# Attention over four images on one core: loads and issues of the start, of each image's first units and of the last group rearranged

## The chip, the cores and the metric

The kernel runs on one core of a Trainium2 chip. The core has five engines with a queue each: PE (TensorE, the matrix engine), ACT (ScalarE), DVE (VectorE), POOL (GpSimd) and SP (SyncE, which here only starts transfers). Transfers (DMAs) started from ACT, SP and POOL share 16 DMA engines. The metric is the device time of one execution in microseconds (us); the median of ten runs is taken.

## The reference

Four images of 64 x 64 points with 256 channels go through one attention layer. `x`, the weights and the result are float32.

```python
B, W, H, C = x.shape            # 4, 64, 64, 256
N = W * H                       # 4096
q = einsum('bwhc,cd->bwhd', x, Wq) + bq      # 128 wide
k = einsum('bwhc,cd->bwhd', x, Wk) + bk      # 128 wide
v = einsum('bwhc,cd->bwhd', x, Wv) + bv      # 256 wide
pq, pk, pv = (t.reshape(B, -1, N) for t in (q, k, v))
energy = einsum('bcn,bcm->bnm', pq, pk)
out = einsum('bcm,bnm->bcn', pv, softmax(energy, axis=-1))
return gamma * out.reshape(B, W, H, C) + x
```

The reshapes make the 4096 columns n and m out of a part of the points and the channels together, which is why q and k pass through DRAM once: they are written in one order and read in another.

## The kernel before

**Exactness.** The large products are made of fp32r matmuls[...]. So each operand is cut into parts: `h` (upper), `l` (rest) and `d` (a scaled combination of both), likewise `vh`, `vl`, `vd` for v and three parts in one tile for q and for k. `halved` (line 245 and on) cuts q or k: one ACT instruction (line 247) and two DVE instructions (line 249). Column 256 of `vh` and `vl` holds ones, so that the accumulators `a0` and `a1`, 258 wide, also collect the softmax's denominator.

**Setting up (lines 84 to 101, 189, 208).** POOL makes `ident`, DVE makes `ones`; ACT's queue starts all weight loads: `wqk_sb` twice, `wv_sb`, `bqk_sb` twice, `bv_sb` twice, `gam`. ACT then scales the bias of v (line 189). DVE puts the ones into `vh` and `vl` (line 208).

**Projection, steps i = 0 to 15 of an image.** A step takes 256 columns: `transposed` (four PE transposes of the x tile, copied from PSUM by ACT, line 129), `project_qk` (eight matmuls, line 136; bias added by DVE, line 145; q parts `qd` and the cut k `kf` stored to DRAM by POOL) and `project_v` of the step before (eight matmuls, line 157; two biased copies by ACT, line 166; `vh` by ACT, line 267; `vl` and `vd` by DVE, line 270). x tiles are loaded by SP, two steps ahead, into three buffers. From step 8 on `begin` brings in the attention's first work: at step 8 `load_q` (SP), at step 9 `halve_q`, at steps 8, 9 and 10 the first three `load_k` (POOL, 768 KB each), from step 10 on half a unit of `energy` per step, at steps 12 to 15 `join` and `upper` of units 0 and 1.

**Attention, units u = 0 to 127 of an image.** A group g has 256 columns n; a unit t, one of eight of a group, takes 512 columns m. For a unit, `energy` makes scores in two halves into the banks `sa` and `sb` (two of each; twelve matmuls, line 303), and ACT takes exponentials of both (line 307, tiles `x` and `y`). `join` multiplies them on DVE (line 317), `upper` makes `h` on ACT (line 322), `halves` makes `l` (line 328) and `d` (line 331) on DVE. `attend` (line 351) multiplies `h`, `l`, `d` with `vh`, `vl`, `vd` into `a0`, `a1` and `bb`: 24 matmuls. Unit t uses the v blocks that steps t and t + 8 made.

The program is written out in the order in which each engine runs it; the framework adds the waits but does not reorder inside the main part. In the loop over units, energies run three units ahead (`LOOK = 3`), `join` and `upper` two units and `halves` one unit ahead:

```python
for k in range(2):
    if ahead < STEPS:
        energy(b, ahead, k)
    if k == 0 and u + 2 < STEPS:
        join(b, u + 2)
        upper(b, u + 2)
load_k(b, ahead + 2)
proceed()
if u + 1 < STEPS:
    halves(b, u + 1)
```

Ahead of the loop stand `halves(b, 0)` and then `project_v(b, NI - 1)`, after the whole of step 15.

**End of a group.** `whole` takes the denominators (line 368) and joins `o` (copied from `bb` by ACT, line 361) with the accumulators (line 371). `finish` is cut into pieces by `yield`; each `proceed()` runs one piece: factors (lines 378, 379) and scaling by ACT (line 381), later four transposes (line 389), later the addition to the x tile (line 393) and the store by POOL (line 394). At the end of an image `while active: proceed()` runs all that is left, ahead of the next image's third transpose.

**End of the program.** All denominators are checked (lines 474 to 481): if one is out of range, a flag sends the program into a general version behind `tc.If`, which does not run with these inputs. All engines read the flag and jump over it.

Of the kernel before, what the change touches and what calls it, by code (L numbers as in the profile page):

```python
# [9 lines left out]
F32 = mybir.dt.float32  # L10
F32R = mybir.dt.float32r
I32 = mybir.dt.int32
AF = mybir.ActivationFunctionType
# [7 lines left out]
def kernel(  # L21
# [67 lines left out]
    wqk_sb = const.tile([P, KC, 2 * C2], F32, name="wqk_sb")  # L89
    nc.scalar.dma_start(wqk_sb[:, :, :C2], wq.rearrange("(k p) d -> p k d", p=P))  # L90
    nc.scalar.dma_start(wqk_sb[:, :, C2:], wk.rearrange("(k p) d -> p k d", p=P))
    wv_sb = const.tile([P, KC, C], F32, name="wv_sb")
    nc.scalar.dma_start(wv_sb, wv.rearrange("(k p) e -> p k e", p=P))
    bqk_sb = const.tile([P, 2 * C2], F32, name="bqk_sb")
    nc.scalar.dma_start(bqk_sb[:, :C2], bq.partition_broadcast(P))
    nc.scalar.dma_start(bqk_sb[:, C2:], bk.partition_broadcast(P))
    bv_sb = const.tile([P, KC], F32, name="bv_sb")
    for eh in range(KC):
        nc.scalar.dma_start(bv_sb[:, eh : eh + 1], bv[eh * P : (eh + 1) * P].unsqueeze(1))
    gam = const.tile([P, 1], F32, name="gam")  # L100
    nc.scalar.dma_start(gam, gamma.partition_broadcast(P))

    class Projection:

# [72 lines left out]
    NU = NM // 4  # L177
    STEPS = NG * NU
    LOOK = 3
    E = 2.0**-12  # L180


    UPPER = 1.0 - 2.0**-13

    again = const.tile([P, 1], I32, name="again")

    zall = const.tile([P, B * NG, NJ], F32, name="zall")
    bv4_sb = const.tile([P, KC], F32, name="bv4_sb")
    nc.scalar.mul(bv4_sb, bv_sb, 1.0 / E)

    with ExitStack() as fast:
        fast.enter_context(tc.manual_schedule())
# [8 lines left out]
        ps_t = pool("ps_t", 1, space=PSUM)  # L201


        vh = qkv.tile([P, NM, C + 2], F32R, tag="vh", name="vh")
        vl = qkv.tile([P, NM, C + 2], F32R, tag="vl", name="vl")
        vd = qkv.tile([P, NM, C], F32R, tag="vd", name="vd")
        for t in (vh, vl):
            nc.vector.tensor_copy(t[:, :, C:], ones[:, : 2 * NM].rearrange("p (m t) -> p m t", t=2))

        images, qd, kf, units, loads, now = [], {}, {}, {}, {}, {}  # L210

# [41 lines left out]
        def project_qk(b, i):  # L253
            images[b].qk(i)
            x = now["qk"]
            for s in range(2):
                nc.gpsimd.dma_start(qd[b, i // 2 + NG // 2 * s][:, i % 2, :], x[:, s, :C2])
            f = kpool.tile([P, 2, 3, P], F32R, tag="f", name=f"f_{b}_{i}", bufs=2)
            halved(f, x[:, :, C2:])
            nc.gpsimd.dma_start(kf[b, i // 2][:, i % 2], f.rearrange("p s j d -> p s (j d)"))  # L260

        def project_v(b, i):
            images[b].v(i)
            v4 = now["v4"]
            m = slice(2 * i, 2 * i + 2)
            h = vh[:, m, :C]
            nc.scalar.activation(h, v4, AF.Identity, scale=UPPER * E)  # L267

            for t, f in ((vl, 1.0 / E), (vd, 1.0 / E + 1.0)):
                nc.vector.scalar_tensor_tensor(  # L270
                    t[:, m, :C], h.bitcast(F32), -f, v4, ALU.mult, ALU.add
                )
# [6 lines left out]
        def halve_q(b, g):  # L279
            t = work.tile([P, NJ, 3, P], F32R, tag="q", name=f"q_{b}_{g}")  # L280
            halved(t, loads.pop((b, "qr", g)))
            loads[b, "q", g] = t

        def load_k(b, u):
            if u < STEPS:
                t = kpool.tile([P, 4, 3, P], F32R, tag="k", name=f"k_{b}_{u}")
                nc.gpsimd.dma_start(t.rearrange("p (i s) f d -> p i s (f d)", s=2), kf[b, u % NU])  # L287
                loads[b, "k", u] = t
# [47 lines left out]
        def attend(b, u, j):  # L336
            g, t = divmod(u, NU)
            if t == j == 0:
                now["acc"] = [
                    ps_o.tile([P, C + 2], F32, tag=f"a{j}", name=f"a{j}_{b}_{g}")  # L340
                    for j in range(NJ)
                ]
                now["bb"] = ps_o.tile([P, NJ, C], F32, tag="bb", name=f"bb_{b}_{g}")
            h, l, d = units[b, u]
            a, bb = now["acc"][j], now["bb"]
            n = slice(j * P, (j + 1) * P)
            for out_, left, right in ((a, h, vh), (a, l, vl), (bb[:, j, :], d, vd)):
                for i in range(4):
                    m = 2 * t + i // 2 + NI * (i % 2)

                    nc.tensor.matmul(  # L351
                        out_,
                        left[:, i, n],
                        right[:, m, :],
                        start=(t == i == 0 and (left is h or left is d and j == 0)),
                        stop=(t == NU - 1 and i == 3 and left is not h),
                        skip_group_check=True,
                    )
            if t == NU - 1 and j == NJ - 1:
                now["o"] = work.tile([P, NJ, C], F32, tag="o", name=f"o_{b}_{g}")  # L360
                nc.scalar.copy(now["o"], bb)

        def whole(b, g):

            o = now["o"]
            for j in range(NJ):
                a = now["acc"][j]
                nc.vector.tensor_copy(zall[:, b * NG + g, j : j + 1], a[:, C : C + 1])
            for j in range(NJ):
                a = now["acc"][j]  # L370
                nc.vector.scalar_tensor_tensor(
                    o[:, j, :], a[:, :C], 1.0 + E, o[:, j, :], ALU.mult, ALU.add
                )

        def finish(b, g, o, xr):
            yield
            r = work.tile([P, NJ], F32, tag="r", name=f"r_{b}_{g}")
            nc.vector.reciprocal(r, zall[:, b * NG + g, :])
            nc.vector.tensor_tensor(r, r, gam.to_broadcast([P, NJ]), ALU.mult)  # L379
            for j in range(NJ):  # L380
                nc.scalar.activation(  # L381
                    o[:, j, :], o[:, j, :], AF.Identity, scale=r[:, j : j + 1]
                )
            yield
            yield
            tp = ps_t.tile([P, 2, NB], F32, tag="t", name=f"ot_{b}_{g}")
            for s in range(2):
                for j in range(NJ):
                    nc.tensor.transpose(  # L389
                        tp[:, s, j * P : (j + 1) * P], o[:, j, s * P : (s + 1) * P], ident  # L390
                    )
            yield
            nc.vector.tensor_tensor(xr, xr, tp, ALU.add)
            nc.gpsimd.dma_start(ov[b, g], xr)

        def begin(b, i):

            if i == 8:
                load_q(b, 0)
            if i == 9:  # L400
                halve_q(b, 0)
            if 8 <= i <= 10:
                load_k(b, i - 8)
            if i >= 10:
                energy(b, (i - 10) // 2, i % 2)
            if i in (12, 14):
                join(b, i // 2 - 6)
            if i in (13, 15):
                upper(b, i // 2 - 6)
                load_k(b, i // 2 - 3)  # L410

        image(0)
        for b in range(B):
# [6 lines left out]
            for i in range(1, NI):  # L420
                if i == 3:
                    now["banks"] = outputs
                if i + 1 < NI:
                    pr.transposed(i + 1)
                begin(b, i)
                project_qk(b, i)
                project_v(b, i - 1)
                proceed()
            halves(b, 0)
            project_v(b, NI - 1)  # L430
            for u in range(STEPS):
                g, t = divmod(u, NU)
# [22 lines left out]
                    halves(b, u + 1)  # L455
                if ahead // NU + 1 < NG and ahead % NU == 5:
                    halve_q(b, ahead // NU + 1)
                for j in range(NJ):
                    attend(b, u, j)
                if t == NU - 1:  # L460
                    whole(b, g)
                    start(finish(b, g, now["o"], loads.pop((b, "x", g))))
                proceed()
            if b + 1 < B:
                images[b + 1].transposed(1)
                project_qk(b + 1, 0)
            while active:
                proceed()


    zs = const.tile([P, 1], F32, name="zs")
    zf = zall.rearrange("p n j -> p (n j)")
    ok = const.tile([P, B * NG * NJ], F32, name="ok")
    nc.vector.tensor_scalar(ok, zf, Z_LOW, None, ALU.is_ge)
    nc.vector.scalar_tensor_tensor(ok, zf, Z_HIGH, ok, ALU.is_le, ALU.mult)
    nc.vector.tensor_reduce(zs, ok, AX.X, ALU.min)
    nc.vector.tensor_scalar(zs, zs, 0.5, None, ALU.is_lt)
    with tc.tile_pool(name="ps_z", bufs=1, space=PSUM) as ps_z:
        zp = ps_z.tile([P, 1], F32, name="zp")
        nc.tensor.matmul(zp, ones, zs, start=True, stop=True)  # L480
        nc.vector.tensor_copy(again, zp)

    NB = 512
    NG = N // NB
# [132 lines left out]
```

## Time and profile before

| what | value |
|---|---|
| median of 10 runs | 2520.88 us (2518.69 to 2523.57) |
| the profiled execution's own time | 2521.07 us |
| its span, first to last instruction | 2518.9 us |
| PE busy | 2486.1 us, 99% |
| DVE busy | 2103.6 us, 84% |
| ACT busy | 1806.4 us, 72% |
| POOL busy | 425.1 us, 17% |
| mean granted PE clock | 0.998 |
| DMA moved | 498.92 MB, 198 GB/s |

The profile shows one execution. A row of the timeline gives the start in us from the span's start, the duration, the engine, the line in the kernel, the instruction, result and operands, the number of instructions put together in the row, and in brackets the idle time before it with what ended that. `PEld` is PE's loading of weights, which runs beside its matmuls. A row of the waits gives the engine and line that waited, what it waited for, and the sum, the number and the longest of these waits. The engine's busy rows divide the span into 40 equal slices and give the busy share in tenths. The time of the run is a little longer than the span, by what lies around the first and the last instruction.

### The profile page before, as it was taken

The page shows a single profiled execution, that of the slowest core. Times are in us where ns is not written, and L with a number is a line of the kernel's source. Part 1 is how long each engine was busy: PE and PEld are TensorE (multiplying, and loading weights), DVE is VectorE, ACT ScalarE, POOL GpSimd, SP SyncE. Part 2 cuts the span into 40 slices and gives each one's busy share as a digit, 9 for nine tenths or more (in the row PEclk, how much of TensorE's full clock was granted, in tenths as well). Part 3 has the DMA queues.
Part 4 walks back from the last instruction along what each step waited for, and adds up shares of the span by engine and source line. Part 5 has one row for each costly group of instructions (what it writes and reads, how often), then busy time and mean ns, then how long its engine had stood idle before and what let it go on. Part 6 is the DMA issues. An engine that isn't in the chain of part 4 may idle for free.

```text
span 2518.9 us, 49987 instructions
## 1 busy us (share of the span) xinstructions
PE 2486.1 (99%) x19970; PEld 2439.6 (97%) x19970; DVE 2103.6 (84%) x2440; ACT 1806.4 (72%) x3138; POOL 425.1 (17%) x774
## 2 busy tenths in 40 slices
PE   8999999999999999999999999999999999999998
PEld 7999999999899999999989999999998999999998
DVE  4888888888688888888868888888886888888887
ACT  4777777777577777777667777777766777777775
POOL 3211111111311111111041111111114111111110
PEclk9999999999999999999999999999999999999999
DMA  6666666665666666666476666666647666666663
GB/s 211 209 208 199 205 197 194 207 204 159 223 211 194 209 198 208 198 192 204 145 240 210 196 200 207 199 204 197 192 144 243 210 206 191 205 200 207 199 197 100
DMA packets 137967, 498.92 MB, mean 198 GB/s; under 512 B 15872, under 2 KB 57856, under 8 KB 137728
## 3 DMA queue, kind: packets, MB, share of 16 engines
q0 software_dynamic: 92160, 453.03, 57.0%
q1 hardware_dynamic: 44032, 41.96, 5.6%
q8 instruction: 160, 2.62, 0.4%
q10 hardware_dynamic: 1536, 0.66, 0.1%
q14 instruction: 79, 0.65, 0.1%
HBM read 445.25 MB, written 50.33 MB: 197 GB/s over the span
## 4 chain that ended last, share of the span: by engine, by line
PE 91%; issue 3%; ACT 3%; DVE 2%; DMA 1%; POOL 0%; POOLq 0%; ACTq 0%; DVEq 0%
PE a L351 38%; PE bb L351 19%; PE sa L303 18%; PE sb L303 10%; PE qk L136 2%; PE v L157 2%; PE ot L389 1%; ACT v L166 1%; DMA k<-kf 1%; ACT vh L267 1%; DVE qks L145 1%; PE xt L123 1%; DVE vd L270 0%; ACT f L247 0%; DMA bv_sb<-in_L_conv_bv_dram 0%
## 5 line engine op out<-in xcount | busy, mean ns | idle before, releaser
L307 ACT ACTIVATE x<-sa 128x512 f32<-128x512 f32 x1024 | 608.6, 594 | 430.7 <-PE sa L303 421.6
L317 DVE TENSOR_TENSOR x<-x,y 128x1024 f32<-128x1024 f32 x512 | 625.6, 1222 | 165.3 <-ACT y L307 165.3
L303 PE MATMUL sa<-q,k 128*128 128x256 f32 x4096 | 744.8, 280 | 7.9 <-ACT x L307 4.1
L351 PE MATMUL a<-vh,h 128*128 128x258 f32 x4096 | 666.5, 285 | 0.0
L351 PE MATMUL a<-vl,l 128*128 128x258 f32 x4096 | 659.8, 283 | 1.7 <-DVE l L328 1.7
L351 PE MATMUL bb<-vd,d 128*128 128x256 f32 x4096 | 650.7, 281 | 1.8 <-DVE d L331 1.8
L303 PEld LDWEIGHTS sa<-q,k 128*128 128x128 f32 x4096 | 622.9, 189 | 10.0 <-ACT x L307 5.0
L328 DVE TENSOR_TENSOR l<-x,h 128x1024 fp32r<-128x1024 f32 x512 | 624.2, 1219 | 0.0
L331 DVE SCALAR_TENSOR_TENSOR d<-h,x 128x1024 fp32r<-128x1024 f32 x512 | 623.9, 1219 | 0.0
L307 ACT ACTIVATE y<-sb 128x512 f32<-128x512 f32 x1024 | 613.1, 599 | 0.0
L303 PE MATMUL sb<-q,k 128*128 128x256 f32 x2048 | 576.2, 281 | 0.0
L351 PEld LDWEIGHTS a<-vl,l 128*128 128x128 f32 x4096 | 563.1, 189 | 2.6 <-DVE l L328 2.6
L322 ACT ACTIVATE h<-x 128x1024 fp32r<-128x1024 f32 x512 | 543.2, 1061 | 29.1 <-DVE x L317 29.1
L351 PEld LDWEIGHTS a<-vh,h 128*128 128x128 f32 x4096 | 560.4, 190 | 1.1
L351 PEld LDWEIGHTS bb<-vd,d 128*128 128x128 f32 x4096 | 556.5, 188 | 2.6 <-issue 2.0
L287 POOL DMA_DIRECT2D k<-kf x512 | 283.5, 554 | 1487.1 <-PE sb L303 1466.9
L303 PEld LDWEIGHTS sb<-q,k 128*128 128x128 f32 x2048 | 384.6, 188 | 8.9 <-ACT y L307 1.0
L136 PE MATMUL qk<-wqk_sb,xts 128*128 128x256 f32 x512 | 123.8, 385 | 4.3 <-ACT xts L129 4.3
L157 PE MATMUL v<-xts,wv_sb 128*128 128x256 f32 x512 | 120.3, 379 | 0.0
L381 ACT ACTIVATE o<-o,r 128x256 f32<-128x256 f32 x128 | 58.3, 503 | 73.9 <-DVE r L379 73.9
L157 PEld LDWEIGHTS v<-xts,wv_sb 128*128 128x128 f32 x512 | 97.3, 190 | 13.2
L136 PEld LDWEIGHTS qk<-wqk_sb,xts 128*128 128x128 f32 x512 | 94.1, 194 | 15.3 <-ACT xts L129 4.7
(41 smaller groups left out, 876.5 us busy)
## 6 DMA issues: line engine op xcount, KB each, us to landing
k<-kf POOLq DMA_DIRECT2D x512, 768.0 KB, 4.7
x<-in_x_dram SPq DMA_DIRECT2D x128, 256.0 KB, 3.5
kf<-f POOLq DMA_DIRECT2D x64, 384.0 KB, 3.7
out_dram<-x POOLq DMA_DIRECT2D x64, 256.0 KB, 2.6
qd<-qks POOLq DMA_DIRECT2D x128, 64.0 KB, 2.2
qr<-qd SPq DMA_DIRECT2D x64, 128.0 KB, 3.0
wv_sb<-in_L_conv_Wv_dram ACTq DMA_DIRECT2D x1, 256.0 KB, 5.0
wqk_sb<-in_L_conv_Wq_dram ACTq DMA_DIRECT2D x1, 128.0 KB, 2.2
```

Source lines behind the costliest of these rows:

```text
L123: nc.tensor.transpose(tp[:, k, s, :], self.xs[i][:, s, k * P : (k + 1) * P], ident,)
L136: nc.tensor.matmul(qk[:, s, :], self.xt[i][:, k, s, :], wqk_sb[:, k, :], start=(k == 0), stop=(k == KC - 1),)
L157: nc.tensor.matmul(vp[:, eh, :], wv_sb[:, k, eh * P : (eh + 1) * P], self.xt[i][:, k].rearrange("p s a -> p (s a)"), start=(k == 0), stop= ...
L287: nc.gpsimd.dma_start(t.rearrange("p (i s) f d -> p i s (f d)", s=2), kf[b, u % NU])
L303: nc.tensor.matmul(to[:, i], kt[:, 2 * k + i, f, :], q[:, :, f, :], start=first, stop=last)
L307: nc.scalar.activation(to[:, 2 * k : 2 * k + 2, :], sp.rearrange("p i j d -> p i (j d)"), AF.Exp, scale=scale,)
L317: nc.vector.tensor_tensor(x, x, y, ALU.mult)
L322: nc.scalar.activation(h, units[b, u], AF.Identity, scale=UPPER)
L328: nc.vector.tensor_tensor(l, x, h.bitcast(F32), ALU.subtract)
L331: nc.vector.scalar_tensor_tensor(d, h.bitcast(F32), 1.0 + E, x, ALU.mult, ALU.subtract)
L351: nc.tensor.matmul(out_, left[:, i, n], right[:, m, :], start=(t == i == 0 and (left is h or left is d and j == 0)), stop=(t == NU - 1 and ...
L381: nc.scalar.activation(o[:, j, :], o[:, j, :], AF.Identity, scale=r[:, j : j + 1])
```

## The change

Ten places differ.

1. Of the loads of the start only `wqk_sb` stays on ACT's queue; `bqk_sb`, `wv_sb`, `bv_sb` and `gam` go to POOL's. POOL also scales the bias of v. ACT, not DVE, fills the columns of ones.
2. Twelve transposes of `ident` into a PSUM tile that nobody reads stand at the head of PE's queue.
3. `vh` and `vl` have rows of 260 numbers (`VC`), not 258; the matmuls still read 258.
4. `load_k` of units 0, 1 and 2 moves from steps 8, 9, 10 to steps 4, 6, 8, `load_q` from step 8 to step 5.
5. `halves(b, 0)` moves into step 15, ahead of `project_v(b, 14)`.
6. `project_v` is split: the biased copies stay, and for the last two blocks of an image the making of `vh`, `vl`, `vd` (`halve_v`) moves into units 1 and 3.
7. What is left of an image's last group runs in step 1 of the next image, behind the third transpose, no longer at the end of the image.
8. The last group of the last image has a function of its own, `finish_last`, which scales out of `bb`, combines, transposes and adds in two blocks of 128 columns; the store is issued by SP.
9. The check of the denominators becomes `guard`, whose pieces stand between those of `finish_last`.
10. `whole` and `finish` share `sums` and `factors` with it.

```diff
     nc.scalar.dma_start(wqk_sb[:, :, C2:], wk.rearrange("(k p) d -> p k d", p=P))
+    bqk_sb = const.tile([P, 2 * C2], F32, name="bqk_sb")
+    nc.gpsimd.dma_start(bqk_sb[:, :C2], bq.partition_broadcast(P))
+    nc.gpsimd.dma_start(bqk_sb[:, C2:], bk.partition_broadcast(P))
     wv_sb = const.tile([P, KC, C], F32, name="wv_sb")
-    nc.scalar.dma_start(wv_sb, wv.rearrange("(k p) e -> p k e", p=P))
-    bqk_sb = const.tile([P, 2 * C2], F32, name="bqk_sb")
-    nc.scalar.dma_start(bqk_sb[:, :C2], bq.partition_broadcast(P))
-    nc.scalar.dma_start(bqk_sb[:, C2:], bk.partition_broadcast(P))
+    nc.gpsimd.dma_start(wv_sb, wv.rearrange("(k p) e -> p k e", p=P))
...
-        nc.scalar.dma_start(bv_sb[:, eh : eh + 1], bv[eh * P : (eh + 1) * P].unsqueeze(1))
+        nc.gpsimd.dma_start(bv_sb[:, eh : eh + 1], bv[eh * P : (eh + 1) * P].unsqueeze(1))
...
-    nc.scalar.dma_start(gam, gamma.partition_broadcast(P))
+    nc.gpsimd.dma_start(gam, gamma.partition_broadcast(P))
...
+    VC = C + 4
...
-    nc.scalar.mul(bv4_sb, bv_sb, 1.0 / E)
+    nc.gpsimd.tensor_scalar(bv4_sb, bv_sb, 1.0 / E, None, ALU.mult)
+
+
+    with tc.tile_pool(name="ps_w", bufs=1, space=PSUM) as ps_w:
+        wp = ps_w.tile([P, P], F32, name="wp")
+        for _ in range(12):
+            nc.tensor.transpose(wp, ident, ident)
...
-        vh = qkv.tile([P, NM, C + 2], F32R, tag="vh", name="vh")
-        vl = qkv.tile([P, NM, C + 2], F32R, tag="vl", name="vl")
+        vh = qkv.tile([P, NM, VC], F32R, tag="vh", name="vh")
+        vl = qkv.tile([P, NM, VC], F32R, tag="vl", name="vl")
...
-            nc.vector.tensor_copy(t[:, :, C:], ones[:, : 2 * NM].rearrange("p (m t) -> p m t", t=2))
+            nc.scalar.copy(t[:, :, C : C + 2], ones[:, : 2 * NM].rearrange("p (m t) -> p m t", t=2))
...
         def project_v(b, i):
             images[b].v(i)
-            v4 = now["v4"]
+            units[b, "v4", i] = now["v4"]
+            if i < NI - 2:
+                halve_v(b, i)
+
+        def halve_v(b, i):
+            v4 = units.pop((b, "v4", i))
             m = slice(2 * i, 2 * i + 2)
...
-                        right[:, m, :],
+                        right[:, m, : out_.shape[1]],
...
-            if t == NU - 1 and j == NJ - 1:
+            if t == NU - 1 and j == NJ - 1 and (b, g) != (B - 1, NG - 1):
                 now["o"] = work.tile([P, NJ, C], F32, tag="o", name=f"o_{b}_{g}")
                 nc.scalar.copy(now["o"], bb)
...
+        def factors(b, g):
+
+            r = work.tile([P, 2, NJ], F32, tag="r", name=f"r_{b}_{g}")
+            nc.vector.reciprocal(r[:, 0, :], zall[:, b * NG + g, :])
+            nc.vector.tensor_tensor(r[:, 0, :], r[:, 0, :], gam.to_broadcast([P, NJ]), ALU.mult)
+            return r[:, 0, :], r[:, 1, :]
...
+        def guard():
+
+            z = zall.rearrange("p n j -> p (n j)")
+            ok = ppool.tile([P, 4, NB], F32, tag="y", name="ok")[:, 0, : B * NG * NJ]
+            nc.vector.tensor_scalar(ok, z, Z_LOW, None, ALU.is_ge)
+            nc.vector.scalar_tensor_tensor(ok, z, Z_HIGH, ok, ALU.is_le, ALU.mult)
+            yield
+            nc.vector.tensor_reduce(zs, ok, AX.X, ALU.min)
+            nc.vector.tensor_scalar(zs, zs, 0.5, None, ALU.is_lt)
+            zp = ps_s.tile([P, 1], F32, tag="b", name="zp")
+            nc.tensor.matmul(zp, ones, zs, start=True, stop=True)
+            yield
+            nc.vector.tensor_copy(again, zp)
+            yield
+            yield
+
+        def finish_last(b, g, xr):
+
+            sums(b, g)
+            r, ra = factors(b, g)
+            check = guard()
+            nc.vector.tensor_scalar(ra, r, 1.0 + E, None, ALU.mult)
+            o = work.tile([P, NJ, C], F32, tag="o", name=f"o_{b}_{g}")
+            tps = []
+            for j in range(NJ):
+                next(check)
+                nc.scalar.activation(
+                    o[:, j, :], now["bb"][:, j, :], AF.Identity, scale=r[:, j : j + 1]
+                )
+                nc.vector.scalar_tensor_tensor(
+                    o[:, j, :], now["acc"][j][:, :C], ra[:, j : j + 1], o[:, j, :], ALU.mult, ALU.add
+                )
+                tp = (ps_t, ps_s)[j].tile([P, 2, P], F32, tag="ta"[j], name=f"ot_{b}_{g}_{j}")
+                for s in range(2):
+                    nc.tensor.transpose(tp[:, s, :], o[:, j, s * P : (s + 1) * P], ident)
+                tps.append(tp)
+            for j in range(NJ):
+                next(check)
+                n = slice(j * P, (j + 1) * P)
+                nc.vector.tensor_tensor(xr[:, :, n], xr[:, :, n], tps[j], ALU.add)
+            nc.sync.dma_start(ov[b, g], xr)
+
         def begin(b, i):
 
-            if i == 8:
+            if i == 5:
                 load_q(b, 0)
             if i == 9:
                 halve_q(b, 0)
-            if 8 <= i <= 10:
-                load_k(b, i - 8)
+            if i in (4, 6, 8):
+                load_k(b, i // 2 - 2)
...
                 if i + 1 < NI:
                     pr.transposed(i + 1)
+                while i == 1 and active:
+                    proceed()
                 begin(b, i)
                 project_qk(b, i)
+                if i == NI - 1:
+                    halves(b, 0)
                 project_v(b, i - 1)
                 proceed()
-            halves(b, 0)
             project_v(b, NI - 1)
...
+                if u in (1, 3):
+                    halve_v(b, NI - 2 + u // 2)
                 for j in range(NJ):
                     attend(b, u, j)
-                if t == NU - 1:
+                if (b, u) == (B - 1, STEPS - 1):
+                    finish_last(b, g, loads.pop((b, "x", g)))
+                elif t == NU - 1:
...
-            while active:
-                proceed()
```

More of the change, by code (lines that the diff above doesn't have):

```diff
@@ L185 @@
     again = const.tile([P, 1], I32, name="again")
+    zs = const.tile([P, 1], F32, name="zs")
     zall = const.tile([P, B * NG, NJ], F32, name="zall")
     bv4_sb = const.tile([P, KC], F32, name="bv4_sb")
-    nc.scalar.mul(bv4_sb, bv_sb, 1.0 / E)
+    nc.gpsimd.tensor_scalar(bv4_sb, bv_sb, 1.0 / E, None, ALU.mult)
[3 more added lines that the diff above has]
+            nc.tensor.transpose(wp, ident, ident)
     with ExitStack() as fast:
@@ L358, in attend, with sums @@
                     )
-            if t == NU - 1 and j == NJ - 1:
+            if t == NU - 1 and j == NJ - 1 and (b, g) != (B - 1, NG - 1):
                 now["o"] = work.tile([P, NJ, C], F32, tag="o", name=f"o_{b}_{g}")
                 nc.scalar.copy(now["o"], bb)
-        def whole(b, g):
-            o = now["o"]
+        def sums(b, g):
             for j in range(NJ):
@@ L368, in whole @@
                 nc.vector.tensor_copy(zall[:, b * NG + g, j : j + 1], a[:, C : C + 1])
+        def factors(b, g):
[3 more added lines that the diff above has]
+            return r[:, 0, :], r[:, 1, :]
+        def whole(b, g):
+            o = now["o"]
+            sums(b, g)
             for j in range(NJ):
@@ L376, in finish @@
             yield
-            r = work.tile([P, NJ], F32, tag="r", name=f"r_{b}_{g}")
-            nc.vector.reciprocal(r, zall[:, b * NG + g, :])
-            nc.vector.tensor_tensor(r, r, gam.to_broadcast([P, NJ]), ALU.mult)
+            r, _ = factors(b, g)
             for j in range(NJ):
@@ L394, in finish @@
             nc.gpsimd.dma_start(ov[b, g], xr)
+        def guard():
[13 more added lines that the diff above has]
+        def finish_last(b, g, xr):
+            sums(b, g)
+            r, ra = factors(b, g)
[20 more added lines that the diff above has]
+            nc.sync.dma_start(ov[b, g], xr)
         def begin(b, i):
-            if i == 8:
+            if i == 5:
                 load_q(b, 0)
@@ L466 @@
                 project_qk(b + 1, 0)
-            while active:
-                proceed()
[L471 to L481, printed above, removed]
     NB = 512
```

## The prediction

> **What bounds the kernel now.** I read the busy rows and the chain that ended last, then the waits of the matrix engine (PE), then the timeline wherever a wait stands.
>
> ```profile
> PE   8999999999999999999999999999999999999998
> ...
> PE 91%; issue 3%; ACT 3%; DVE 2%; DMA 1%; POOL 0%; POOLq 0%; ACTq 0%; DVEq 0%
> ```
>
> PE is the bound from the second slice to the last but one, and 91% of the chain. The change takes no matmul of the main loop away, so what it can win is time in which PE stands still or runs slowly. The waits of PE say where:
>
> ```profile
> PE xt L123 <- DMA x<-in_x_dram: 5.4, 2, 4.4
> PE qk L136 <- ACT xts L129: 4.3, 1, 4.3
> PE sa L303 <- ACT x L307: 4.1, 4, 1.1
> PE sa L303 <- DMA k<-kf: 3.8, 3, 1.9
> PE bb L351 <- DVE d L331: 1.8, 4, 0.5
> PE a L351 <- DVE l L328: 1.7, 4, 0.4
> ```
>
> The first two belong to the start; the others recur once per image. These are small: all PE idle time is 2518.9 - 2486.1 = 32.8 us. Because the modelled end of a matmul overlaps the next, a wait costs more than its row says. So I measure the cost as start to start, against the usual pitch: 0.120 us for an `a` matmul, 0.118 for `bb`, 0.114 for `sa` and `sb`, 0.216 for `qk` and `v`, 0.109 for a transpose.
>
> **1. Start.** The timeline of the first 20 us:
>
> ```profile
> 4.41 1.09 PE L123 MATMUL xt<-ident,x 128*128 128x128 f32 x4 [4.41 <-DMA x<-in_x_dram]
> ...
> 9.91 1.28 ACT L189 ACT_TABLE_LOAD   x1 [9.91 <-DMA gam<-in_L_conv_gamma_dram]
> ...
> 11.93 3.78 PE L136 MATMUL qk<-wqk_sb,xts 128*128 128x256 f32 x8 [4.29 <-ACT xts L129]
> ...
> 18.96 1.89 PE L157 MATMUL v<-xts,wv_sb 128*128 128x256 f32 x8
> ```
>
> ACT sits behind its own weight loads and the scaled bias (line 189, which waits until 9.9 for `bv`), so the first copy of a transposed x comes at 11.3. Then eight `qk` matmuls take 3.78 us where the same eight take 1.89 at 18.96: PE runs at half speed, and the clock record turns to full at 18.1.
>
> After: ACT issues two loads (until 1.7), loads its table (1.28, to 3.0) and fills the ones columns (0.32 + 0.18 on DVE today, to some 3.5), all before the first copy is due. POOL takes six issues at 0.54 to 0.7 each, and in the built order the first (`bq`) stands ahead of the instruction that finishes `ident`; that is then ready at about 1.9, not 1.3. Twelve half-speed transposes (0.213 each) run 1.95 to 4.5, the first x (4.4) is transposed to 5.4 and copied by 6.0. Next in PE's order is the second x, landed at 6.5 today with `wv` in competition; I take 6.0 (5.5 to 6.6). Four pieces remain before the first `v`: xt 0.44, qk 1.73, xt 0.44, qk 1.73 = 4.34 us at full speed, against 18.96 today. The POOL loads hide behind this: `bqk` must land by about 9.5, `wv` by 12, `bv` by 13; POOL's own DMAs land 2.2 to 4.7 us after issue, so `bv`, issued at about 4, comes in time. Without that cover each us late is a us lost.
>
> Here the clock decides. The Trainium skill (TensorE: Matmul & The Clock Gate, Part 1, What's actually happening) says that one busy window of about 3.4 us releases the throttle, on a free-running window. If the twelve transposes count as busy, full speed comes by 6 and `v` starts at 10.4: gain 8.6. The row speaks against that: PE was busy from 11.93 and full speed came 6.2 us later, so a window with some idle in it did not count, and after the change there are still holes at about 5.4 to 6.0. Then the window starts anew at 6.0, full speed comes between 9.4 and 12.8 (the phase is chance), `v` at 12.0 to 13.7. I take 12.7: gain **6.3**, ends 5.0 and 8.6.
>
> **2. First k loads.** Before, three loads of 768 KB are issued at steps 8, 9 and 10, among the stores of `qd` and `kf` and the x loads, and take 6.5 to 7.9 us to land (median of all k loads 4.7). The first `sa` of an image is late, start to start, by 0.48, 0.23, 1.87 and 2.19 us: 4.8 in all. At steps 4, 6 and 8 (their `kf` rows are stored by steps 1, 3, 5, one step of 3.9 us or more earlier, against 3.7 to land) each has six steps, over 20 us, until its unit's first score (steps 10, 12, 14). On POOL's queue they stand before that step's `qd` and `kf` stores, whose users come later; on SP's queue `load_q` stands between two x loads and waits for stores three steps old. Gain **4.8**, ends 4.0 and 5.0.
>
> **3. l and d sooner, last two v halvings later.** The first units of image 0:
>
> ```profile
> 82.40 1.22 DVE L328 TENSOR_TENSOR l<-x,h 128x1024 fp32r<-128x1024 f32 x1
> ...
> 83.53 1.22 DVE L331 SCALAR_TENSOR_TENSOR d<-h,x 128x1024 fp32r<-128x1024 f32 x1
> ...
> 83.67 0.75 PE L351 MATMUL a<-vl,l 128*128 128x258 f32 x4 [0.43 <-DVE l L328]
> ...
> 84.67 0.69 DVE L270 SCALAR_TENSOR_TENSOR vl<-vh,v 128x512 fp32r<-128x512 f32 x1
> ...
> 84.90 0.72 PE L351 MATMUL bb<-vd,d 128*128 128x256 f32 x4 [0.47 <-DVE d L331]
> ...
> 85.87 1.22 DVE L317 TENSOR_TENSOR x<-x,y 128x1024 f32<-128x1024 f32 x1
> ...
> 87.12 1.06 ACT L322 ACTIVATE h<-x 128x1024 fp32r<-128x1024 f32 x1 [1.19 <-DVE x L317]
> ...
> 88.72 0.50 PE L303 MATMUL sa<-q,k 128*128 128x256 f32 x2 [0.99 <-ACT x L307]
> ```
>
> DVE is behind: `l` waits for four `vl`/`vd` of the last v blocks, PE waits for `l`, `d`, and later, through join, `h` and the exponential of line 307, for a score bank. From the first weight load of the first unit (82.48) to that of the second (89.67) is 7.19 us; a unit is 4.29 (24 `a`/`bb` at 0.120 = 2.88, energy 4 x 0.35 = 1.41). Lost: 2.9 per image.
>
> After, with start-to-start pitches on DVE of 1.14 (large) and 0.60 (v half), on ACT of 0.49 (exponential) and 0.96 (`h`): `l` runs 80.4 to 81.6, `d` to 82.8, PE asks for them at 83.0 and 83.4: no wait. join 82.7 to 83.9, `h` to 85.0, second exponential to 85.5; PE asks for that bank at 82.48 + 2.88 + 0.70 = 86.06: no wait. What was skipped comes back: in unit 1 `vh` stands behind unit 4's exponentials on ACT (89.3 to 89.9), `vl` and `vd` hold DVE until 91.2 (0.5 idle, 1.2 of work), in unit 2 the q halves take 0.72, in unit 3 the last v block again idles and works about 1.8. DVE needs 3.42 of each 4.29, so it wins back only 0.87 per unit. Carried forward, PE asks for a score bank in unit 5 at 103.2 and gets it at 103.6: a wait of 0.43 for `sa` and 0.26 for `sb`, 0.7 in all. Then it is clear. Saved 2.9 - 0.7 = 2.2 per image, x4 = **8.8**. If nothing is paid back it is 11.6; if every later ACT and DVE step is 0.05 slower, the late wait is about 1.7 and it is 4.8.
>
> **4. Drain of a finished image moved behind the third transpose.**
>
> ```profile
> 636.72 3.82 SPq L82 DMA_DIRECT2D x<-in_x_dram  x2
> ...
> 638.59 0.95 PE L389 MATMUL ot<-ident,o 128*128 128x128 f32 x4 [0.17 <-ACT o L381]
> ...
> 639.37 0.60 PE L123 MATMUL xt<-ident,x 128*128 128x128 f32 x4
> ```
>
> Today PE does the `ot` transposes from 638.59, in the shadow of the x load issued at 636.72; that lands after 2.6 us, and `xt` starts at 639.37. After, `xt` comes first, stands from 638.26 until the same 639.37, and `ot` follows with 4 x 0.109 = 0.44. A loss of 0.44 at three image changes: **-1.3** (ends -1.6 and, should the load be early, +1.0).
>
> **5. End.**
>
> ```profile
> 2511.05 0.70 POOL L394 DMA_DIRECT2D out_dram<-x  x1 [26.12 <-DVE x L393]
> ```
>
> Before: last `bb` ends at 2506.65, then copy, two combinations, factors, two scalings, four transposes, add (to 2510.75), the store, landed at 2514.3. POOL's closing drain runs 2511.76 to 2518.11, all others wait for it, end 0.8 later. After, from rows of the same shapes: factors to 2506.75 on DVE, first scaling out of the accumulator (0.50) to 2507.3, combination 0.41 behind the two guard steps to 2507.9, transposes to 2508.3; second block, behind reduce 0.29 and compare 0.15, combined at 2508.7, transposed at 2509.1, added by 2509.7, and the SP issue there: 1.3 us sooner. POOL holds no store and takes its drain from about 2509.5. If that lasts the same 6.35, the end is 2.2 sooner; if it lasts only while POOL has DMAs out, SP is last (issue 0.6, read of the flag 0.5, jump 2.7, its semaphores 1.4: about 2514.9) and the end 3.3 sooner. I take **2.8**, ends 1 and 5.
>
> **6. Rows of `vh` and `vl` 1,040 bytes apart, not 1,032.** The Trainium skill (SBUF — State Buffer, Specifications) says that SBUF has 16-byte lines and each crossing costs. A row of 258 numbers that starts 8 bytes into a line, as every odd one does today, touches 66 lines, not 65. At one part in 65 of 0.120 us that is 1.8 ns for 4096 of the 8192 `a` matmuls: 7.5 us. The rows: `a` on odd rows has a pitch 1.8 ns above that on even rows, `bb`, whose rows all start on a line, shows 0.9 in the same positions; the rest is 0.9 ns x 4096 = 3.6. Positions of `bb` differ among themselves from 113 to 123 ns, so that contrast may be chance. I take half the row, **2.0**; ends -4 (new addresses, new collisions) and 7.5.
>
> **Sum.** 6.3 + 4.8 + 8.8 - 1.3 + 2.8 + 2.0 = 23.4. The profiled execution took 2521.07, of which 2518.9 are the span; that is 0.2 above the median of 2520.88. So 2520.9 - 23.4 = **2497.5**. The twelve transposes, the extra multiply and the split sums lie in idle time and cost nothing; were the load of x at once, the transposes would cost up to 2.6.
>
> **Rivals.** (A) As above, 0.65; its own range is 2491 to 2503.
> (B) The wait only moves: ACT's `vh` at the end of unit 1 and 3 and DVE's repayment hold PE in units 2 to 5 for almost what was saved. For it: DVE is busy 18.66 of 20 us in that stretch, and only 0.9 us come free per unit. Against it: with the same pitches the kernel before comes out at 3.1 lost, where 2.9 are measured. Part 3 is then worth 1, the time 2505. 0.15.
> (C) The start is warm (8.6), the row spacing pays by the rule (7.5), the late wait is nought (11.6): 8.6 + 4.8 + 11.6 - 1.3 + 2.8 + 7.5 = 34, time 2487. 0.14.
> (D) Slower: the new spacing puts the `a` rows where they collide with the weight loads that run beside them. The gain without part 6 is 21.4, so it decides from 21.4 / 8192 = 2.6 ns per `a` matmul. Today single positions lie 3 to 6 ns above the mean, so the size exists; that the mean goes there does not follow. At 6 ns: +49 - 21, time 2549. 0.04.
> (E) The k loads moved do nothing, since the banks or POOL hold step 10 as well: 2502, inside A's neighbourhood. 0.02.
>
> **Range and chances.** A and most of B and C lie in 2486 to 2507; left out are D and the tails of C and B, less than 2 in 10. No change within 0.2% (5 us, which is about what a measurement can tell) needs nearly all parts to fail at once: 0.02. Slower 0.04, faster 0.94.
>
> **What would show it.** First `v` at about 12.7 and no ACT table load after 3 us; no PE wait for `k`; no wait for `l` or `d` in the first unit, a wait of under 1 us for a score bank in units 4 to 6; `xt` waiting 1.1 us for x at each image change; SP's store at about 2509.7; a pitch of odd-row `a` matmuls near the even ones. I am wrong if PE waits for `sa` by more than 2 us per image, or if the pitch of `a` or `bb` moves by over 1 ns (8 to 12 us).

## The result, and the profile after

The changed kernel takes **2500.83 us** (median of 8 executions, 2499.52 to 2502.23), the kernel before beside it 2521.3 us (28 executions): a ratio of 0.9919, 95% interval 0.9911 to 0.9928. That is 20.5 us, or 0.8%, faster; 23.4 had been forecast (2497.5). The profiled execution after took 2502.37 us, of which 2500.6 are the span, so it is 1.5 us above its median, where the one before (2521.07) lay close to its own. One of the 28 executions before took 4942.95 us; no trace of it was kept, and the ratio is that of the fast runs. The two spans differ by 18.3 us, and these are accounted for here.

The busy rows, the chain that ended last and, whole, the list of PE's waits of the kernel after:

```profile
PE 2486.6 (99%) x19982; PEld 2444.6 (98%) x19982; DVE 2103.3 (84%) x2440; ACT 1806.5 (72%) x3138; POOL 424.6 (17%) x780
...
PE 95%; ACT 2%; DMA 1%; DVE 1%; issue 1%; POOL 0%; SPq 0%; ACTq 0%; DVEq 0%; POOLq 0%
```

```profile
PE wp L197 <- POOL ident masks.py:199: 2.4, 1, 2.4
PE ot L451 <- DVE o L446: 1.5, 1, 1.5
PE xt L123 <- DMA x<-in_x_dram: 1.4, 1, 1.4
```

PE's idle time fell from 32.8 to 2500.6 - 2486.6 = 14.0 us. All that recurred once per image (`k`, `l`, `d`, the score bank) is gone from PE's own list; what remains stands in the start and the end. The weight loads (PEld) are listed apart, and two small recurring waits are hidden there, as will be seen.

The stages, cut at the same matmuls in both traces and measured start to start:

| stage | before, us | after, us | gain over all | forecast |
|---|---|---|---|---|
| span's start to first `v` matmul | 18.96 | 13.62 | 5.3 | 6.3 |
| first `v` to first `sa`, four images | 33.70, 33.45, 35.10, 35.41 | 33.22 each | 4.8 | 4.8 |
| first `sa` to the end of the last `v` block | 28.5 each | 28.52, 29.11, 29.17, 28.52 | -1.25 | 0 |
| unit 0 to unit 1 | 7.19 each | 4.28, 4.28, 4.29, 4.38 | 11.5 | 11.6 |
| unit 4 to unit 5 | 4.23 each | 4.86, 4.87, 4.87, 4.83 | -2.5 | -2.8 |
| units 16 to 127 | 478.85, 479.15, 478.87, 478.39 | 479.26, 479.28, 479.26, 478.84 | -1.4 (-1.7 with all stretches not listed, units 5 to 16 above all) | 2.0 |
| first `qk` of an image to its first `v`, three seams | 5.01 each | 4.76 each | 0.75 | -1.3 |
| last `bb` to the end | 12.58 | 11.15 | 1.4 | 2.8 |

With the -1.7 they sum to 18.3. So the two parts that were forecast from measured pitches (k loads, first units) came out to 0.2 us, and the others missed by 1 to 4 us each, all but the seam downwards.

**The start.** The timeline of the first 14 us after; columns are start, length, engine, line and instruction, in brackets the idle time ahead of it and what ended it:

```profile
1.27 0.68 POOL L93 DMA_DIRECT2D bqk_sb<-in_L_conv_bq_dram  x1 [0.34 <-issue]
...
2.42 2.82 PE L197 MATMUL wp<-ident 128*128 128x128 f32 x12 [2.42 <-POOL ident masks.py:199]
...
6.45 0.59 ACT L129 COPY xts<-xt 128x512 f32<-128x512 f32 x1 [3.05 <-PE xt L123]
7.81 0.71 PEld L123 LDWEIGHTS xt<-ident,x 128*128 128x128 f32 x4 [1.80 <-DMA x<-in_x_dram]
...
8.72 2.90 PE L136 MATMUL qk<-wqk_sb,xts 128*128 128x256 f32 x8
...
13.62 0.59 PE L157 MATMUL v<-xts,wv_sb 128*128 128x256 f32 x2
```

ACT's first copy comes at 6.45 in place of 11.3, as meant. The twelve transposes end at 5.24, when the first x has already landed (4.0), so its own transposes start only at 5.30; behind them PE waits all the same, for the second x, which lands at 7.8. I had taken 6.0, and before it was 6.5. The clock record turns to full at 10.76, inside the first `qk` block.

**The late wait.** Around unit 4 of image 0:

```profile
93.56 0.69 DVE L283 SCALAR_TENSOR_TENSOR vl<-vh,v 128x512 fp32r<-128x512 f32 x1 [0.41 <-ACT vh L280]
...
94.17 0.69 DVE L283 SCALAR_TENSOR_TENSOR vd<-vh,v 128x512 fp32r<-128x512 f32 x1
...
94.77 1.22 DVE L330 TENSOR_TENSOR x<-x,y 128x1024 f32<-128x1024 f32 x1
...
96.08 1.06 ACT L335 ACTIVATE h<-x 128x1024 fp32r<-128x1024 f32 x1 [1.58 <-DVE x L330]
...
97.68 0.30 PEld L316 LDWEIGHTS sa<-q,k 128*128 128x128 f32 x2 [0.26 <-ACT x L320]
...
98.16 0.19 PEld L316 LDWEIGHTS sb<-q,k 128*128 128x128 f32 x1 [0.19 <-ACT y L320]
```

This is the debt of the skipped `v` blocks as the forecast described it: DVE idles 0.41 for `vh`, makes `vl` and `vd`, joins late, ACT's `h` idles 1.58 for that join, the exponential behind it frees the bank late, and PE stands for `sa` and then `sb`. It costs 0.63 us per image where 0.7 was worked out.

**A new wait**, in images 1 and 2 only:

```profile
648.62 0.54 POOL L268 DMA_DIRECT2D kf<-f  x1 [0.37 <-issue]
...
656.34 0.42 ACT L255 ACTIVATE f<-qks 128x256 fp32r<-128x256 f32 x1 [3.14 <-DMA kf<-f]
...
667.40 0.19 PEld L316 LDWEIGHTS sa<-q,k 128*128 128x128 f32 x1 [0.29 <-DVE q L257]
```

The store of `kf` issued at 648.62, behind the first k load on POOL's queue, takes 7.4 us to land by the chain (the median of all these stores is 4.0). `f` has two buffers, so ACT stands 3.1 us for one of them at 656.34; DVE gets its inputs late, and its q halves are being made while the first score already asks for them. PE's second `sa` is 0.6 us late.

**The seam between images:**

```profile
628.96 1.89 PE L136 MATMUL qk<-wqk_sb,xts 128*128 128x256 f32 x8
629.15 2.71 SPq L82 DMA_DIRECT2D x<-in_x_dram  x2
...
630.69 0.60 PE L123 MATMUL xt<-ident,x 128*128 128x128 f32 x4
...
631.13 0.84 PE L410 MATMUL ot<-ident,o 128*128 128x128 f32 x4
...
631.89 1.99 PE L136 MATMUL qk<-wqk_sb,xts 128*128 128x256 f32 x8
```

`xt` starts right behind the eight `qk`, 1.54 us after SP's issue and without a wait for x. That load, which landed at 632.14, was not this tile's.

**The end.**

```profile
2489.10 0.64 PE L364 MATMUL bb<-vd,d 128*128 128x256 f32 x4
...
2492.22 0.83 DVE L456 TENSOR_TENSOR x<-x,ot 128x256 f32<-128x256 f32 x2
2493.07 0.60 SPq L457 DMA_DIRECT2D out_dram<-x  x1
```

The store goes out 3.6 us after the start of the last `bb` matmul (2489.45, the fourth of its row), before 4.7 us after it. POOL starts its closing drain at the same moment, 2493.07, and is in it until 2499.75; SP is through at 2498.7, so POOL still ends last.

### The profile page after: what moved, and what is told of

It reads as the page before. It is cut to its first block, busy times and chain, and to the rows that moved or that the text cites. A ratio compares the mean times of both kernels' runs of the same rounds, so it can differ in the third digit from the quotient of the medians.

```text
span 2500.6 us, 50025 instructions
## 1 busy us (share of the span) xinstructions
PE 2486.6 (99%) x19982; PEld 2444.6 (98%) x19982; DVE 2103.3 (84%) x2440; ACT 1806.5 (72%) x3138; POOL 424.6 (17%) x780
## 4 chain that ended last, share of the span: by engine, by line
PE 95%; ACT 2%; DMA 1%; DVE 1%; issue 1%; POOL 0%; SPq 0%; ACTq 0%; DVEq 0%; POOLq 0%
PE a L364 39%; PE bb L364 19%; PE sa L316 19%; PE sb L316 10%; PE qk L136 3%; PE v L157 3%; PE ot L410 1%; DMA kf<-f 1%; PE xt L123 1%; ACT h L335 1%; DVE x L330 0%; ACT x L320 0%; ACT vh L280 0%; DMA x<-in_x_dram 0%; DVE vd L283 0%
## 5 line engine op out<-in xcount | busy, mean ns | idle before, releaser
L136 PEld LDWEIGHTS qk<-wqk_sb,xts 128*128 128x128 f32 x512 | 93.1, 192 | 10.8 <-ACT xts L129 0.5
```

The costliest lines, as they stand in the source:

```text
L136: nc.tensor.matmul(qk[:, s, :], self.xt[i][:, k, s, :], wqk_sb[:, k, :], start=(k == 0), stop=(k == KC - 1),)
```

## The experiments

Each was profiled once and timed beside the kernel before, whose median was then 2520.93 us. The account by stages is called theory A: parts 2 and 3 each bring what their stages show, whether or not the other is there; the row spacing brings nothing; the rest of the miss is at the start and the end.

**Part 3 alone, in the kernel before.**

```diff
 def project_v(b, i):
     images[b].v(i)
-    v4 = now["v4"]
+    units[b, "v4", i] = now["v4"]
+    if i < NI - 2:
+        halve_v(b, i)
...
     project_qk(b, i)
+    if i == NI - 1:
+        halves(b, 0)
     project_v(b, i - 1)
     proceed()
-halves(b, 0)
...
+    if u in (1, 3):
+        halve_v(b, NI - 2 + u // 2)
```

> The kernel before with part 3 alone: l and d of the first unit of each image in step 15, the last two v blocks halved in units 1 and 3. Theory A (the parts add up as the stages show): first to second unit 7.2 -> 4.3 us in every image, fourth to fifth unit 4.23 -> 4.85, no wait for the q halves before the first score, so 4 x (2.9 - 0.6) = 9.2 us sooner, about 2512.1. Rival B (the wait only moves when the k loads stay late): under 4 us sooner, 2517 or more, with PE waits for a score bank in units 2 to 5 that eat the rest.

Measured: 2510.18 us, ratio 0.9955 (0.9942 to 0.9969), 10.8 us sooner by medians; 8.8 by spans (the profiled execution lies 1.7 above its median). Unit 0 to 1 is 4.22 us in every image, unit 4 to 5 4.85 to 4.88, so 11.9 - 2.5 = 9.4 from part 3. No `l`, `d` or bank wait is left among PE's waits, here all of them, while the k loads still are:

```profile
PE xt L123 <- DMA x<-in_x_dram: 5.6, 2, 4.3
PE sa L308 <- DMA k<-kf: 4.7, 3, 2.0
PE qk L136 <- ACT xts L129: 4.3, 1, 4.3
PE ot L394 <- ACT o L386: 1.6, 4, 1.1
PE zp L488 <- DVE zs L485: 1.0, 1, 1.0
```

The last `v` block comes 28.52 us after the first `sa` in all four images: part 3 doesn't cause the new wait. Rival B of the forecast (the wait only moves, gain 1 us) is excluded: 8.8 remain after the debt is paid.

**Part 2 alone, in the kernel before.**

```diff
-if i == 8:
+if i == 5:
     load_q(b, 0)
...
-if 8 <= i <= 10:
-    load_k(b, i - 8)
+if i in (4, 6, 8):
+    load_k(b, i // 2 - 2)
```

> The kernel before with part 2 alone: k loads at steps 4, 6, 8 and the q load at step 5. Theory A: the four first scores come 33.2 us after the first v (33.7, 33.45, 35.1, 35.4 before), 4.8 us sooner; and if these loads are what makes the stores of kf slow and so the q halves late, images 1 and 2 show the 0.6 us between the first score and the last v block here too: net 3.6, about 2517.7. Rival: the late q halves come from the other parts of the change, then none of it here: 4.8 sooner, about 2516.5.

Measured: 2515.51 us, ratio 0.9977 (0.9968 to 0.9986); 5.4 us sooner by medians, 4.9 by spans. The first `sa` comes 33.22 us after the first `v` in all four images, 4.8 in all, and no `k` row stands among PE's waits, again all of them:

```profile
PE qk L136 <- ACT xts L129: 5.8, 1, 5.8
PE xt L123 <- DMA x<-in_x_dram: 4.2, 1, 4.2
PE sa L303 <- ACT x L307: 4.0, 4, 1.1
PE bb L351 <- DVE d L331: 1.8, 4, 0.5
PE a L351 <- DVE l L328: 1.7, 4, 0.4
PE ot L389 <- ACT o L381: 1.6, 4, 1.1
PE zp L480 <- DVE zs L477: 1.0, 1, 1.0
```

The part of theory A that put the late q halves down to these loads alone fell: 28.52 us in all four images, as the rival had it, so the 1.25 us are not here. But their first link is. ACT's wait for a buffer of `f`, in the lists of all waits, before and with part 3 alone absent, with part 2 alone 6.4 us, after 12.0 us:

```profile
ACT f L247 <- DMA kf<-f: 6.4, 4, 1.9
```

```profile
ACT f L255 <- DMA kf<-f: 12.0, 5, 3.2
```

So with the early k loads the stores of `kf` do stop ACT. The slowest of them are no slower than before, when one issued at 680.34, behind the k load of step 10, took 7.8 us to land and nobody waited for it. Here ACT stands for at most 1.9 us, which is made good before the first score, and after for up to 3.2, which isn't. What makes it longer after was not isolated. A kernel with the first q halves one step sooner, which would test the last link, was not tried.

**Rows 258 apart again, in the kernel after.**

```diff
-VC = C + 4
+VC = C + 2
```

> The kernel after with rows of 258 numbers (1,032 bytes) in vh and vl again. As predicted (rows that start on a line are cheaper): 2.0 us slower, 2502.8. If the new spacing costs what the steady stretches show (0.1 to 0.45 us per image, 1.4 in all): 1.4 faster, 2499.4, with a mean a+bb+score pitch per image of 478.9 in place of 479.26 us between units 16 and 127. If it does nothing: 2500.8, and the 479.26 stays.

Measured: 2499.69 us, ratio to before 0.9913 (0.99 to 0.9927), which the times can't tell from 0.9919. The trace can. Units 16 to 127 take 478.83, 478.84, 478.78 and 478.41 us in place of 479.26, 479.28, 479.26 and 478.84: 1.8 us sooner with the old spacing. The new wait is gone in image 1 (28.53) and 0.44 in image 2 (28.96), though ACT's waits for `f` are much the same (10.5 us in five, the longest 3.0); so its size is not a matter of the order of the program alone. Against that stands a start 1.4 us longer, though nothing in it was changed:

```profile
7.72 1.11 PE L123 MATMUL xt<-ident,x 128*128 128x128 f32 x4 [1.31 <-DMA x<-in_x_dram]
8.41 3.11 PEld L136 LDWEIGHTS qk<-wqk_sb,xts 128*128 128x128 f32 x8
8.62 3.62 PE L136 MATMUL qk<-wqk_sb,xts 128*128 128x256 f32 x8
...
12.89 2.31 PE L136 MATMUL qk<-wqk_sb,xts 128*128 128x256 f32 x8
...
15.04 1.24 PE L157 MATMUL v<-xts,wv_sb 128*128 128x256 f32 x5
```

All eight `qk` of the first block run at half speed here; the clock record turns to full at 13.73, where it did at 10.76 after. The same start, 0.1 us apart at the first `qk`, got full speed 3.0 us apart.

**Rows 260 apart, alone in the kernel before** (the closing test of the denominators then stands inside the main part, in a tile of another pool, for want of room).

```diff
-vh = qkv.tile([P, NM, C + 2], F32R, tag="vh", name="vh")
-vl = qkv.tile([P, NM, C + 2], F32R, tag="vl", name="vl")
+vh = qkv.tile([P, NM, C + 4], F32R, tag="vh", name="vh")
+vl = qkv.tile([P, NM, C + 4], F32R, tag="vl", name="vl")
...
-    right[:, m, :],
+    right[:, m, : out_.shape[1]],
```

> The kernel before with rows of 260 numbers (1,040 bytes) in vh and vl alone (the closing test of the sums works in a tile of another pool, inside the main part, for want of room). As predicted: 2.0 us faster, 2519.3. If the spacing costs: 1.4 slower, 2522.7, with 479.26 in place of 478.9 us between units 16 and 127. If it does nothing: 2521.3. The closing part may move by some tenths, as its test is issued elsewhere; the stretches decide.

Measured: 2523.98 us, ratio 1.001 (1.0001 to 1.0019), 3.0 us slower. Three things make up the span's 3.6 us. The stretch from unit 16 to 127 gives 1.2 (479.19, 479.46, 479.13, 478.69), and units 5 to 16 another 0.3. The moved closing test makes the end 1.5 longer (14.10 in place of 12.58), which was taken for some tenths. And the first `sa` of image 3 comes late by 2.2 us as before, but is followed by 3.41 us at half clock. By stretches (length, PE busy, granted clock, DMA share, GB/s):

```profile
1921.00:1923.50 2.50, 0.55 (x6) 1.00 1.01 318
1923.50:1925.00 1.50, 1.50 (x10) 0.99 1.17 435
1925.00:1928.40 3.40, 3.40 (x10) 0.50 1.10 397
1928.40:1932.00 3.60, 3.60 (x23) 1.00 0.99 338
```

PE had stood 1.95 us for `k`; a little later the clock fell, at 1924.96 to 1928.38, and ten matmuls ran in a stretch that holds twenty in the kernel before, where the same wait had no such consequence. That cost 1.7 us. It was traced once, but the eleven executions of this kernel suggest that it is frequent: the five with a mean granted clock of 0.997 took 2524.41 to 2525.74 us, the six with 0.998 took 2521.67 to 2523.98. Against these three stand 0.3 us at the start and 0.8 at the `k` waits of the other images, which came out shorter.

The row spacing is thus confirmed from both sides, by adding it (+1.2) and by taking it away (-1.8), to be a loss. The four stretches from unit 16 to 127 together take 1914.9 to 1915.3 us in the four kernels with rows of 258 and 1916.5 and 1916.6 in the two with rows of 260, so the difference is clear of their spread. The steady stretches, all pitches start to start and summed over the four images' units 16 to 126, tell where:

| matmuls | before | rows of 260 alone | after | after, rows of 258 |
|---|---|---|---|---|
| `a`, 7104 | 860.8 us | 855.2 us | 856.0 us | 860.7 us |
| `bb`, 3552 | 419.1 us | 422.9 us | 422.8 us | 419.1 us |
| `sa` and `sb`, 5184 | 614.3 us | 617.4 us | 617.0 us | 614.0 us |

The `a` matmuls did become cheaper, by 4.7 to 5.6 us. The others, which read neither `vh` nor `vl`, took more than that back. For the scores that is 0.6 ns each in the mean. It shows in the median duration of one `sa` too, the middle one of three times (min/median/max in ns), before and with rows of 260 alone:

```profile
L303 PE MATMUL sa<-q,k x4096: 276/276/469, 52.7 to 2494.8; 128*128 128x256 f32 x196
```

```profile
L304 PE MATMUL sa<-q,k x4096: 276/281/469, 51.9 to 2496.7; 128*128 128x256 f32 x196
```

and after, and after with rows of 258:

```profile
L316 PE MATMUL sa<-q,k x4096: 276/281/469, 46.8 to 2477.8; 128*128 128x256 f32 x196
```

```profile
L316 PE MATMUL sa<-q,k x4096: 276/276/469, 48.3 to 2476.6; 128*128 128x256 f32 x196
```

Two tiles that are 256 bytes longer per partition also move what lies behind them. Whether the spacing itself or the new place of the other tiles slows `bb` and `sa` isn't told apart by these runs: a kernel with rows of 258 in tiles of the larger size would tell, and was not tried.

## Why the prediction was right, and where it wasn't

The total is 3.3 us off the median, inside the range, and the likeliest case (A) is the one that came: two thirds of the gain is parts 2 and 3, which both hold alone. The working of the other four parts was wrong in size or in sign, and they cancel in part. By the spans the miss is 5.1 us, not 3.3, and it would be 7 without the seam, which came out better than forecast for a reason that the forecast did not have: that much is luck.

1. **Start: mechanism right, 1.0 us too high.** The term that failed is "I take 6.0 (5.5 to 6.6)" for the second x: it landed at 7.8. That PE stood waiting for it is shown. That the loads moved to POOL's queue make it late is the reading of six traces: between 4.0 and 6.5 us the DMA engines moved 143 GB/s here and 140 with rows of 258, against 269 to 291 in the four kernels that leave these loads on ACT's queue, and the second x landed at 7.8 and 7.7, against 5.4 to 6.7. Which of the loads does it isn't shown; a kernel with the small ones on another queue was not tried. The full clock came at 10.8, inside the forecast's 9.4 to 12.8; that softened the miss. With the clock as it fell in the experiment with rows of 258 (13.7, outside), the gain would have been 18.96 - 15.04 = 3.9 us, below the lower end of 5.0. The Trainium skill (TensorE: Matmul & The Clock Gate, Part 1, What's actually happening) calls the window free-running, so that the same kernel can find a different phase at its start. The two runs agree in that (3.0 us apart); the variation of 0.5 us either way that the section gives for the transition is smaller than what they show. The warm-up transposes didn't bring the 8.6 us of the warm start in either run; what they brought wasn't isolated.

2. **k loads: right**, 4.8 in the change and alone. What was not costed is the queue that they were moved to the front of. I wrote that the stores behind them have users that come later; ACT, which needs the buffer back, was one that comes soon. That is the first link of the 1.25 us in images 1 and 2; part 2 alone has the link and not the loss.

3. **First units: right, step by step**: 11.5 of 11.6 saved, 2.5 of 2.8 paid back, in the unit and through the bank that were named; alone 11.9 and 2.5. Carrying DVE's debt forward in its own pitches was what made the number. All of it is shown by the traces, and that the debt is from the `v` block of unit 3 follows from the order there; putting that block one unit later was not tried.

4. **Seam: wrong sign.** The step that failed is that PE does the `ot` transposes "in the shadow of the x load issued at 636.72". I had taken that issue for the load of the tile transposed at 639.37. But it landed at 639.51, after that tile's transposes had begun, and in the trace of before no wait for x stands at that place; PE there waited for ACT's scaling of `o`, ahead of `ot`. With `xt` first, the first of the two scalings is hidden (the weights of the later `ot` still stand 0.26 us for the second), and each seam is 0.25 us shorter.

5. **End: mechanism right, 1.4 too high.** The store goes out 3.6 us after the start of the last `bb`, 0.3 later than worked out. The larger half is POOL's drain: I had taken a value between one as long as today's and none without stores. It is 6.68 us after, in the kernel with rows of 258 again 6.68, and 6.35 in all four whose last store is POOL's. So it doesn't shrink when POOL has no store out. Nor does it follow the store where there is one: with rows of 260 alone the store is issued 2.3 us ahead of the drain, before 0.7 us, and the drain is 6.35 us long in both. What it waits for isn't shown.

6. **Row spacing: wrong sign.** The Trainium skill's rule of lines crossed (SBUF — State Buffer, Specifications) was weighed against the pitch of `a` alone, and `a` did gain. Two steps failed. One is the count "66 lines, not 65": a row of 1,032 bytes that starts 8 bytes into a line ends at byte 1,040, which is the end of the 65th line, and a row that starts on a line touches 65 too. Counted rightly, the rule promised no gain. The pattern isn't that of odd rows either: with rows of 260 alone, the second and third `vh` matmuls of four gain 1.9 and 2.8 ns and the first and fourth under 0.3, while the odd rows are the third's and the fourth's. The other step is the silent one, that nothing but `a` would change; `bb` moved by 1.0 ns, just over the limit that the forecast had set as a sign of being wrong. Rival D, that it costs more than all else brings, needed 2.6 ns per `a`; the cost is 1.2 to 1.8 us over some 16,000 matmuls, or 0.1 ns each.

Taken together: 23.4 - 1.0 (start) + 0.2 (first units) - 1.25 (q halves) + 2.05 (seam) - 1.4 (end) - 3.7 (spacing) = 18.3. The medians show 20.5, 2.1 more than the spans: the profiled execution after lies 1.5 us above its median, the one before 0.2 below, and 0.4 are won outside the spans. One half-clock window more or less is worth 1.7 us, and the kernel before has two k waits of about 2 us per execution that can bring one on, as seen in one run; that this has a part in the gap between the medians isn't shown.

The fastest version seen is the change with rows of 258; the times don't separate it from the change itself, the stretches do, by 1.8 us.

## What to carry to other kernels

Start-to-start pitches of one engine, carried forward unit by unit, forecast a postponed piece of work within some tenths of a microsecond; sizes read off a row's wait do not. Before a load is moved to the front of a queue, list what is queued behind it and ask of each transfer who needs its buffer back, not only who reads its data. A change of one tile's layout is judged by the pitch of every matmul in the stretch, since the ones that don't touch the tile may pay for it.

## What the runs showed of the hardware

- A wait of 1.95 us on PE was followed by 3.41 us at half clock in one execution and by none in another with the same wait at the same place; the price was 1.7 us. A wait of some two microseconds can therefore cost nearly twice its length; what decides it isn't shown.
- In two kernels that differ only in the spacing of rows, the clock turned full 2.0 and 5.1 us after the first `qk`.
- With the loads of the biases, `wv_sb` and `gam` on POOL's queue the DMA engines moved 140 and 143 GB/s between 4.0 and 6.5 us, with them on ACT's 269 to 291.
- With two tiles that it doesn't read 258 or 260 numbers to a row, the median `sa` matmul took 276 or 281 ns, and its mean pitch with `sb` rose by 0.6 ns.
- POOL's closing drain lasted 6.35 us in four kernels whose last store is POOL's and 6.68 in two whose last store is SP's.
